# A selective-scan kernel: the skip term made in the next chunk's softplus burst, half in the first and half in the third direction, and the third pair's late sums behind its third turn

## The chip, the cores and the metric

The kernel runs on one core of a Trainium2 chip. The metric is device microseconds of one execution. TensorE (PE) multiplies matrices and turns tiles, VectorE (DVE) runs the scans, ScalarE (ACT) does exponentials and scaled copies, GpSimd (POOL) does elementwise products, SyncE (SP) issues DMAs. A product of float32 operands appears in the trace as two passes of PE, a turn (transpose) as one.

## The reference

The input has 8 images of 384 channels and 64 x 64 positions. Layer 0 normalises by groups, runs a channel attention with 1x1 and 3x3 convolutions, and adds the input. Layer 1 is a selective scan with four directions: along the rows, along the columns, and both in reverse.

```python
xs = stack([x0, x1, x0[..., ::-1], x1[..., ::-1]])      # 4 directions, 4096 steps
dts, Bs, Cs = split(einsum('bkdl,kcd->bkcl', xs, x_proj_weight))
dt = softplus(einsum('bkrl,kdr->bkdl', dts, dt_projs_weight) + dt_bias)
# for each step: h = h * exp(dt * A) + (dt * u) * B ;  y = sum over 16 states of h * C
ys = ys + Ds.reshape(K, D)[None, :, :, None] * u        # the skip term
y = y0 + y2 + yt                                        # four directions, merged in place
out = x + gelu(layer_norm(y))
```

All four directions' results are added at the same positions, so the skip term is, at each position, the normalised input times the sum of the four D's. It may be added once, whole or in parts, with any direction's results.

## The kernel before

For each image the attention runs first and then the scan. The scan works on 32 *chunks*: directions k = 0 to 3, and in each 8 pieces of 512 steps, in rising order for k of 0 and 1 and in falling order for 2 and 3. A chunk has 16 states, taken two at a time in 8 *pairs*, p = 0 to 7. Channels are three blocks of 128 partitions.

One call of `period(g)` emits the work of one pair, g counting pairs over all chunks. Everything in it is pinned, so each engine runs exactly in the order in which the Python code emits. A period holds:

- six scans on DVE (`scan`, L569: two states, three channel blocks), each fed by a decay exp(dt*A) made by ACT into PSUM (`decay`, L548, two banks) and by the drive w*B from POOL (`drive`, L557);
- for the pair before, o = g - 1: eight *turns* on PE (`turn`, L591), each three transposes of 64 steps with both states, from h into one of two PSUM banks (`ps_t`); for each turn a scaled copy out of PSUM with C as the scale (`apply_c`, L603 on ACT, L605 on DVE for some); and after every two copies a sum over the two states (`add_up`, L626 and L632), products with the constant `pair` that accumulate in `py`, three PSUM banks that live through the chunk;
- the projections of the chunk two ahead (`project`, L455), and POOL's `weigh` and `keep_last`.

Sums come in four quarters of 128 steps, lb = 0 to 3. The first three write 384 channels into the first columns of one bank each. The last (lb = 3, "late sums", twelve passes at L632) goes to the spare 128 columns of all three banks. Its eighth copy is made in the next period, after the first turn, and the sums follow behind the second turn of that next period (`add_up(o - 1, NJ)`), or behind the third turn where `odd` holds. That is the case from the third pair on when the chunk two ahead is in direction 1 or 3, whose input is read with a stride.

The second pair of a chunk, p = 1, is the *burst*. In it the step sizes of the next chunk are made: `step_matmuls` makes three products with 512 columns (L514), two in the banks of the turns and the third, pd0, in the bank `ps_m`. In front of pd0 stands a filler, a product of the same operand with the identity (L513), which pd0 overwrites. Then `step_size` runs three softplus on ACT (L524) between two changes of the activation table. In the burst three of the copies run on DVE, and DVE also takes the finished `py` of the chunk before (`take_all`: L675 copies it in direction 0, L677 adds it to the stored sums of earlier directions) before the next chunk's first sums overwrite it.

The skip term is made in direction 0 only. Twelve products per chunk (L618: a 128 x 128 block of the normalised input, times a diagonal of summed D's) are spread over the pairs by the table `SKIPS`, two with each of pairs 2 to 7, each directly in front of the sums of its quarter. Since pair p's sums are made one period later, and the late ones two periods later, the products run in the periods of p = 3 to 7 and in p = 0 of the next chunk.

```python
SKIPS = {2: (0, 1), 3: (2, 3), 4: (0, 3), 5: (1, 3), 6: (0, 2), 7: (1, 2)}
```

Of the kernel before, what the change touches and what calls it, by code (L numbers as in the profile page):

```python
# [15 lines left out]
P = 128  # L16
C = 384
NJ = C // P
H = W = 64
L = H * W  # L20
CH = 512
# [10 lines left out]
NP = N // 2  # L32
# [1 line left out]
NQ = CH // HP  # L34
PX = 4

SKIPS = {2: (0, 1), 3: (2, 3), 4: (0, 3), 5: (1, 3), 6: (0, 2), 7: (1, 2)}

FT = 256
JUNK = 512  # L40
# [36 lines left out]
def tile_channel_attention_then_selective_scan(ctx: ExitStack, tc: tile.TileContext, a: dict):  # L77
    nc = tc.nc
# [27 lines left out]
    skip = const.tile([P, NJ, P], F32, name="skip")  # L106
# [275 lines left out]
    def selective_scan(b, x1, stats1):  # L382
# [10 lines left out]
        with ExitStack() as st:  # L393
# [6 lines left out]
            pin = tc.keep_in_program_order  # L400
# [11 lines left out]
            with tc.tile_pool(name=f"sn{b}", bufs=1) as np_:  # L412
# [4 lines left out]
                for c in range(NCH):  # L417
                    for j in range(NJ):
                        s = x1[j][:, bass.ts(c, CH)]
# [20 lines left out]
            steps = []  # L440
# [59 lines left out]
                bts[g] = work.tile([P, 2, CH], F32, tag="B", bufs=3, name=f"B{b}_{g}")  # L500
                nc.sync.dma_start(bts[g], bc_ds[s][2 * p : 2 * p + 2, :].partition_broadcast(P))

            def step_matmuls(s):

                k = steps[s][0]
                pds = [None] * NJ
                for j in (1, 2, 0):
                    pool, tag = (ps_m, "m") if j == 0 else (ps_t, "t")  # L510
                    pds[j] = pool.tile([P, CH], F32, tag=tag, name=f"pd{b}_{s}_{j}")
                    if j == 0:
                        pin(nc.tensor.matmul(pds[j], lhsT=ident, rhs=xds[s], start=True, stop=True))  # L513
                    pin(nc.tensor.matmul(  # L514
                        pds[j], lhsT=wdt[:, k, bass.ts(j, P)], rhs=xds[s], start=True, stop=True
                    ))
                return pds
# [18 lines left out]
            das, dbs, h2s, hcs, pts, pys, carries = {}, {}, {}, {}, {}, {}, {}  # L536
# [70 lines left out]
            def add_up(g, lb):  # L607

                s, p = divmod(g, NP)
                if p == 0 and lb == 0:  # L610
                    pys[s] = ps_y.tile([P, NJ, CH], F32, tag="py", name=f"py{b}_{s}")
                hc, py = hcs.pop((g, lb)), pys[s]
                k, c = steps[s][:2]

                if k == 0 and lb in SKIPS.get(p, ()):
                    j = sum(lb in SKIPS[i] for i in SKIPS if i < p)
                    o = py[:, lb, bass.ts(j, P)] if lb < NJ else py[:, j, C:]
                    pin(nc.tensor.matmul(  # L618
                        o, lhsT=x1[j][:, c * CH + lb * P : c * CH + (lb + 1) * P],
                        rhs=skip[:, j, :], start=False, stop=False,  # L620
                    ))

                flags = dict(start=p == 0 and lb < NJ, stop=p == NP - 1 and lb == NJ)
                if lb < NJ:
                    for f in range(2):
                        pin(nc.tensor.matmul(  # L626
                            py[f * HP : (f + 1) * HP, lb, :C], lhsT=pair, rhs=hc[:, f, :], **flags
                        ))
                else:
                    for j in range(NJ):  # L630
                        for f in range(2):
                            pin(nc.tensor.matmul(  # L632
                                py[f * HP : (f + 1) * HP, j, C:], lhsT=pair,
                                rhs=hc[:, f, bass.ts(j, P)], **flags,
                            ))

            def rows(k, c):

# [42 lines left out]
            for s in range(2):  # L681
                for i in range(PX * NJ):
                    project(s, i)
                lay_out(s)
                if s == 0:
                    step_size(0, step_matmuls(0))
                    for j in range(NJ):
                        weigh(0, j)
                    for g in range(3):
                        fetch(g)  # L690
                    drive(0, 0)
                    drive(0, 1)
                    decay(0, 0, 0)
                    decay(0, 0, 1)
            mingle_c(0)

            def period(g):

                o, s, p = g - 1, g // NP, g % NP
                last = g == S * NP
                burst = p == 1 and s + 1 < S
                on_dve = {3, 4, 5} if burst else {0: {2}, 2: {2}}.get(p, set())
                taken = s - 1 if p == 1 and s > 0 else None

                def step(i):  # L710
                    if not last:
                        scan(g, *divmod(i, NJ))

                def next_decay(i, home=None):
                    if not last:
                        decay(g, *divmod(i + 2, NJ), home)

                def apply(q):
                    if o >= 0:
                        apply_c(o, q, nc.vector if q in on_dve else nc.scalar)  # L720

                def turned(q):
                    if o >= 0:
                        turn(o, q)

                def added(lb):
                    if o >= 0:
                        add_up(o, lb)

                def projected(i):  # L730
                    if s + 2 < S:
                        project(s + 2, i)

                def take_all():
                    if taken is not None:
                        for i in range(NJ):
                            take(taken, i)

                if not last:
                    h2s[g] = work.tile([P, NJ, CH, 2], F32, tag="h", bufs=3, name=f"h{b}_{g}")  # L740
                    if p == 2:
                        sum_of(s)
                if o >= 0:
                    keep_last(o)
                fetch(g + 3)
                drive(g + 1, 0)
                if p == 3 and s + 1 < S:
                    mingle_c(s + 1)
                if p in (2, 4, 6) and s + 1 < S:
                    weigh(s + 1, p // 2 - 1)  # L750
                turned(0)
                step(0)
                if o >= 1:
                    apply_c(o - 1, NQ - 1, nc.scalar)
                turned(1)

                odd = p >= 2 and s + 2 < S and steps[s + 2][0] % 2 == 1
                if p >= 3 or odd:
                    projected(2 * p - 4)
                if o >= 1 and not odd:  # L760
                    add_up(o - 1, NJ)
                next_decay(0)
                step(1)
                apply(0)
                turned(2)
                if o >= 1 and odd:
                    add_up(o - 1, NJ)
                next_decay(1)
                step(2)
                drive(g + 1, 1)  # L770
                apply(1)
                if burst:
                    pds = step_matmuls(s + 1)
                    apply(2)
                    next_decay(2)
                    next_decay(3, work)
                    step_size(s + 1, pds)
                    step(3)
                    step(4)
                    take_all()  # L780
                    step(5)
                    turned(3)
                    turned(4)
                    added(0)
                    apply(3)
                    turned(5)
                    apply(4)
                    turned(6)
                    added(1)
                    next_decay(4)  # L790
                    next_decay(5)
                    apply(5)
                    turned(7)
                    added(2)
                    apply(6)
                    return
                turned(3)
                if p == 1:
                    take_all()
                added(0)  # L800
                if p == 0 and 0 < s < S - 1:
                    lay_out(s + 1)
                apply(2)
                turned(4)
                next_decay(2)
                step(3)
                apply(3)
                turned(5)
                added(1)
                next_decay(3)  # L810
                step(4)
                apply(4)
                turned(6)
                apply(5)
                turned(7)
                added(2)
                if p == 2 and not odd:
                    projected(0)
                if p >= 2:
                    projected(2 * p - 3)  # L820
                if p == 0 and s < S:
                    turn_c(s)
                next_decay(4)
                step(5)
                apply(6)
                next_decay(5)
                if p == 0 and s < S:
                    keep_c(s)
# [82 lines left out]
    for b in range(B):  # L911
        x1, x1_d, stats1 = channel_attention(b, *x, before)
# [52 lines left out]
```

## Time and profile before

| | |
|---|---|
| median of 3 runs | 20747.19 us (20741.09 to 20748.04) |
| profiled execution | 20748.06 us, span 20746.3 us |
| busy, share of the span | PE 93%, DVE 93%, ACT 87%, POOL 74%, weight loads 51% |
| mean granted TensorE clock | 0.969 |
| skip products L618 | 1536 passes, 311.8 us busy |
| filler L513 | 512 passes, 263.2 us busy |
| turns L591 | 49152 passes, 7976.9 us busy, idle before them 457.5 us |
| late sums L632 | 24576 passes, 1871.6 us busy |
| scaled copies L603 on ACT | 15128, 8437.0 us busy, idle before them 346.5 us |

Length of each direction in image 1, from the first scan of one direction to that of the next (the last one ends with the first scan of its last pair): 539.67, 518.81, 514.63 and 505.57 us.

An entry "idle before, <- releaser" names the instruction whose end let the engine go on. Ends of PE's passes are modelled, so busy time of PE overlaps; starts are recorded. Times in the timeline count from the span's start.

### The profile page before, as it was taken

To read this page: it belongs to the slowest core of one execution; us is meant where nothing else is said; L and a number is where in the kernel's file an instruction comes from. 1 tells how busy PE (TensorE), PEld (TensorE's weight loads), DVE (VectorE), ACT (ScalarE), POOL (GpSimd) and SP (SyncE) were. 2 spreads that over 40 slices of the span, in tenths; PEclk is the share of its full clock that TensorE was granted. 3 is DMA by queue.
4 is the path that set the end of the run, shared out by engine and by line. 5 is a ranking of instruction groups with operands and counts; after the bars stand their busy time and mean duration, and the time that the engine had idled before them with its cause. 6 is when DMAs were issued, how large, how long until landed. Compare 5 with 4: busy or idle time off the path is not lost. (4 is left out here: it accounts for less than half of the span.)

```text
span 20746.3 us, 319602 instructions
## 1 busy us (share of the span) xinstructions
PE 19205.9 (93%) x118256; PEld 10578.6 (51%) x118256; DVE 19321.9 (93%) x17310; ACT 17951.9 (87%) x32267; POOL 15441.2 (74%) x6918
## 2 busy tenths in 40 slices
PE   7999979999899998999989999899998999989998
PEld 4555545555455554555545555455554555545554
DVE  8999989999899998999989999899998999989998
ACT  3999949999599995999859998599985999859998
POOL 0899808998189981899819997199972999729997
PEclk8999989999899998999989999899998999989999
DMA  1232322323223232232322323223232232322223
GB/s 40 76 92 92 101 77 77 92 93 101 75 80 92 92 104 70 80 92 93 105 68 80 92 92 105 70 80 92 92 103 71 81 93 92 98 74 82 92 92 117
DMA packets 953164, 1807.96 MB, mean 87 GB/s; under 512 B 125905, under 2 KB 646353, under 8 KB 945457
## 3 DMA queue, kind: packets, MB, share of 16 engines
q1 hardware_dynamic: 950736, 1787.40, 27.2%
q8 instruction: 933, 15.29, 0.3%
q14 instruction: 631, 5.16, 0.1%
q10 hardware_dynamic: 864, 0.12, 0.0%
HBM read 1468.39 MB, written 318.77 MB: 86 GB/s over the span
## 5 line engine op out<-in xcount | busy, mean ns | idle before, releaser
L557 POOL TENSOR_TENSOR db<-w,B 128x1536 f32<-128x1536 f32 x4088 | 14143.8, 3467 | 566.6 <-DVE h L569 238.8
L569 DVE TENSOR_TENSOR_SCAN h<-da,ca,db 128x512 f32<-128x512 f32 x10752 | 13058.6, 1267 | 500.2 <-issue 204.3
L603 ACT ACTIVATE hc<-pt,ct 128x384 f32<-128x384 f32 x15128 | 8437.0, 579 | 346.5 <-PE pt L591 287.5
L548 ACT ACTIVATE da<-dt,neg_a 128x512 f32<-128x512 f32 x12288 | 8504.5, 695 | 166.3 <-DVE h L569 134.2
L591 PE MATMUL pt<-ident,h 128*128 128x128 f32 x49152 | 7976.9, 287 | 457.5 <-ACT hc L603 305.0
L591 PEld LDWEIGHTS pt<-ident,h 128*128 128x128 f32 x49152 | 5145.5, 140 | 5115.7 <-ACT hc L603 2549.8
L626 PE MATMUL py<-hc,pair 128*64 128x384 f32 x24576 | 5327.1, 512 | 9.1 <-DVE ys L677 9.1
L406 POOL MEMSET wdt<- 128x1536 f32 x8 | 11.0, 1378 | 3621.5 <-DMA x1d<-x 3621.5
L569 DVE TENSOR_TENSOR_SCAN h<-da,db 128x512 f32<-128x512 f32 x1536 | 1811.5, 1231 | 145.2 <-ACT da L548 75.6
L632 PE MATMUL py<-hc,pair 128*64 128x128 f32 x24576 | 1871.6, 281 | 0.0
L626 PEld LDWEIGHTS py<-hc,pair 128*64 128x64 f32 x24576 | 1216.6, 135 | 1014.6 <-issue 945.3
L455 PE MATMUL px<-x,wx 128*44 128x128 f32 x6144 | 1501.7, 338 | 35.4 <-ACT x L421 29.1
L632 PEld LDWEIGHTS py<-hc,pair 128*64 128x64 f32 x24576 | 1377.2, 136 | 267.2 <-issue 240.2
L532 POOL TENSOR_TENSOR w<-x,dt 128x512 f32<-128x512 f32 x744 | 1057.9, 1422 | 0.0
L455 PEld LDWEIGHTS px<-x,wx 128*44 128x44 f32 x6144 | 635.0, 121 | 817.1 <-issue 771.9
L583 POOL COPY ca<-h 128x6 f32<-128x6 f32 x1792 | 344.2, 192 | 828.4 <-DVE h L569 817.2
L514 PE MATMUL pd<-xd,wdt 128*128 128x512 f32 x1536 | 781.5, 618 | 87.6 <-ACT hc L603 81.8
L605 DVE TENSOR_SCALAR hc<-pt,ct 128x384 f32<-128x384 f32 x1256 | 741.1, 607 | 106.2 <-PE pt L591 61.1
L353 PE MATMUL pp<-v,mT 128*128 128x512 f32 x1152 | 553.9, 634 | 123.5 <-DVE v L244 57.3
L524 ACT ACTIVATE dt<-pd,dt_bias 128x512 f32<-128x512 f32 x768 | 475.4, 686 | 21.3 <-PE pd L514 17.7
L514 PEld LDWEIGHTS pd<-xd,wdt 128*128 128x128 f32 x1536 | 275.3, 192 | 401.3 <-ACT hc L603 199.7
L353 PEld LDWEIGHTS pp<-v,mT 128*128 128x128 f32 x1152 | 228.3, 205 | 403.0 <-issue 312.1
(315 smaller groups left out, 11713.7 us busy)
## 6 DMA issues: line engine op xcount, KB each, us to landing
B<-bcd SPq DMA_DIRECT2D x2048, 512.0 KB
yd<-ys SPq DMA_DIRECT2D x128, 576.0 KB
ys<-yd SPq DMA_DIRECT2D x256, 288.0 KB
yd<-ys SPq DMA_DIRECT2D x256, 288.0 KB
x<-in_x SPq DMA_DIRECT2D x48, 1024.0 KB
x1d<-x SPq DMA_DIRECT2D x192, 256.0 KB
fy<-yd SPq DMA_DIRECT2D x128, 384.0 KB
fin<-yd SPq DMA_DIRECT2D x112, 384.0 KB
```

The costliest lines, as they stand in the source:

```text
L353: nc.tensor.matmul(pc, lhsT=mT[:, j, bass.ts(m, P)], rhs=v[:, j, bass.ts(c, CH)], start=j == 0, stop=j == NJ - 1,)
L455: pin(nc.tensor.matmul(split(pxs[s][:XR, :])[:, part, :], lhsT=wx[:, j, k, :], rhs=view(x1[j], k, c)[:, part, :], start=i == 0, stop=i == ...
L514: pin(nc.tensor.matmul(pds[j], lhsT=wdt[:, k, bass.ts(j, P)], rhs=xds[s], start=True, stop=True))
L532: pin(eng.tensor_mul(split(ws[s][:, j, :]), view(x1[j], k, c), split(dts[s][:, j, :])))
L548: pin(nc.scalar.activation(t, dts[s][:, j, :], AF.Exp, scale=neg_a[:, j, k, n : n + 1]))
L557: pin(eng.tensor_mul(t, ws[g // NP], bts[g][:, v : v + 1, :].broadcast_to([P, NJ, CH])))
L569: pin(nc.vector.tensor_tensor_scan(h, da, db, 0.0 if start else carries[s - 1][:, j, n : n + 1], ALU.mult, ALU.add,))
L591: pin(nc.tensor.transpose(t[:, bass.ts(j, P)], h2s[g][:, j, bass.ts(q, HP), :].rearrange("p l v -> p (l v)"), ident))
L603: pin(eng.activation(out, src, AF.Copy, scale=scale))
L605: pin(eng.tensor_scalar_mul(out, src, scale))
L626: pin(nc.tensor.matmul(py[f * HP : (f + 1) * HP, lb, :C], lhsT=pair, rhs=hc[:, f, :], **flags))
L632: pin(nc.tensor.matmul(py[f * HP : (f + 1) * HP, j, C:], lhsT=pair, rhs=hc[:, f, bass.ts(j, P)], **flags,))
```

## The change

Three things change. `SKIPS` is now keyed by direction: in direction 0 the quarters 0 and 1, in direction 2 the quarters 2 and 3. `add_up` no longer makes skip products; a new function `add_skip` makes the six of a chunk in one go. It is called in the burst of the next chunk, in front of `step_matmuls`, and where it is called, the filler in front of pd0 is left out. The accumulation's last-product flag moves with it. Lastly, `late` extends the order "late sums behind the third turn" to the third pair (p = 2) of every chunk. The number of skip products is the same, 768; the fillers fall from 256 to 128.

```diff
-SKIPS = {2: (0, 1), 3: (2, 3), 4: (0, 3), 5: (1, 3), 6: (0, 2), 7: (1, 2)}
+SKIPS = {0: (0, 1), 2: (2, 3)}
...
-            def step_matmuls(s):
+            def step_matmuls(s, filled):
...
-                    if j == 0:
+                    if j == 0 and not filled:
                         pin(nc.tensor.matmul(pds[j], lhsT=ident, rhs=xds[s], start=True, stop=True))
...
-                if k == 0 and lb in SKIPS.get(p, ()):
-                    j = sum(lb in SKIPS[i] for i in SKIPS if i < p)
-                    o = py[:, lb, bass.ts(j, P)] if lb < NJ else py[:, j, C:]
-                    pin(nc.tensor.matmul(
-                        o, lhsT=x1[j][:, c * CH + lb * P : c * CH + (lb + 1) * P],
-                        rhs=skip[:, j, :], start=False, stop=False,
-                    ))
-
-                flags = dict(start=p == 0 and lb < NJ, stop=p == NP - 1 and lb == NJ)
+                flags = dict(start=p == 0 and lb < NJ, stop=False)
+                open_ = skip_banks(k)
...
+                        flags["stop"] = p == NP - 1 and j not in open_
...
+            def skip_banks(k):
+                return {i for lb in SKIPS.get(k, ()) for i in ([lb] if lb < NJ else range(NJ))}
+
+            def add_skip(s):
+                k, c = steps[s][:2]
+                py = pys[s]
+                places = []
+                for lb in SKIPS[k]:
+                    for j in range(NJ):
+                        bank, o = (lb, py[:, lb, bass.ts(j, P)]) if lb < NJ else (j, py[:, j, C:])
+                        places.append((bank, lb, j, o))
+                for i, (bank, lb, j, o) in enumerate(places):
+                    pin(nc.tensor.matmul(
+                        o, lhsT=x1[j][:, c * CH + lb * P : c * CH + (lb + 1) * P],
+                        rhs=skip[:, j, :], start=False,
+                        stop=bank not in [q[0] for q in places[i + 1 :]],
+                    ))
...
                 odd = p >= 2 and s + 2 < S and steps[s + 2][0] % 2 == 1
+                late = odd or p == 2
                 if p >= 3 or odd:
                     projected(2 * p - 4)
-                if o >= 1 and not odd:
+                if o >= 1 and not late:
                     add_up(o - 1, NJ)
...
                 turned(2)
-                if o >= 1 and odd:
+                if o >= 1 and late:
                     add_up(o - 1, NJ)
...
                 if burst:
-                    pds = step_matmuls(s + 1)
+                    filled = taken is not None and steps[taken][0] in SKIPS
+                    if filled:
+                        add_skip(taken)
+                    pds = step_matmuls(s + 1, filled)
```

Here `taken` is the chunk before, so 16 bursts per image are filled: those of the chunks that follow one of direction 0 or 2.

More of the change, by code (lines that the diff above doesn't have):

```diff
@@ L685, in selective_scan @@
                 if s == 0:
-                    step_size(0, step_matmuls(0))
+                    step_size(0, step_matmuls(0, False))
                     for j in range(NJ):
```

## The prediction

> **What bounds the kernel now.** Most of the span is the selective scan: 2079 of some 2580 us per image. The page gives four engines 74 to 93% of the span, which names no bound, so I read the scan stage in stretches cut at the first scan of each pair. These are pairs 4, 5 and 7 (counted from 0) of a chunk of direction 0 (chunk 3 of image 1), then the same pairs of the last chunk of direction 1. Columns: length, then busy time of PE, weight loads, DVE, ACT and POOL.
>
> ```profile
> core 0: us, PE busy (x) PEld busy (x) DVE busy (x) ACT busy (x) POOL busy (x), PEclk, DMA share, GB/s
> 3307.08:3314.91 7.83, 7.69 (x58) 4.51 (x55) 7.38 (x7) 7.71 (x15) 7.83 (x3) 1.00 0.20 69
> 3314.91:3323.03 8.12, 8.12 (x60) 4.80 (x61) 7.26 (x7) 7.57 (x15) 7.39 (x6) 1.00 0.20 65
> 3331.15:3339.41 8.26, 8.26 (x60) 4.97 (x58) 7.27 (x6) 7.68 (x15) 7.13 (x5) 1.00 0.23 69
> ...
> 4096.63:4104.18 7.55, 7.29 (x54) 4.15 (x56) 7.26 (x6) 7.55 (x15) 7.55 (x3) 1.00 0.18 69
> 4104.18:4111.74 7.56, 7.31 (x54) 4.17 (x56) 7.27 (x6) 7.56 (x15) 7.41 (x4) 1.00 0.24 73
> 4119.29:4126.85 7.56, 7.31 (x54) 4.16 (x56) 7.32 (x7) 7.56 (x15) 7.31 (x3) 1.00 0.24 73
> ```
>
> In direction 1 ACT is busy for the whole period and sets it at 7.56 us. In direction 0, where the skip term lies in these periods, PE fills pairs 5 and 7, ACT has holes, and the period is 0.3 to 0.7 us longer. The timeline of pair 5 in direction 0 shows the hole (start, length, engine, instruction, idle before):
>
> ```profile
> 3318.50 0.87 PE L591 MATMUL pt<-ident,h 128*128 128x128 f32 x6
> 3319.14 0.58 ACT L603 ACTIVATE hc<-pt,ct 128x384 f32<-128x384 f32 x1 [0.55 <-PE pt L591]
> ...
> 3320.34 2.46 DVE L569 TENSOR_TENSOR_SCAN h<-da,ca,db 128x512 f32<-128x512 f32 x2 [0.63 <-ACT da L548]
> ```
>
> The fourth turn comes late behind two skip products, ACT stands 0.55 us, its next decay is late, DVE stands 0.63 us. The same place in direction 1 has PE waiting for ACT instead:
>
> ```profile
> 4107.92 0.55 PE L591 MATMUL pt<-ident,h 128*128 128x128 f32 x3 [0.17 <-ACT hc L603]
> ```
>
> Now the burst, the second pair, in direction 2:
>
> ```profile
> 4266.79 1.99 PE L514 MATMUL pd<-xd,wdt 128*128 128x512 f32 x4 [0.33 <-ACT hc L603]
> 4267.08 1.35 ACT L548 ACTIVATE da<-dt,neg_a 128x512 f32<-128x512 f32 x2
> ...
> 4268.45 1.28 ACT L524 ACT_TABLE_LOAD   x1
> 4268.61 1.02 PE L513 MATMUL pd<-xd,ident 128*128 128x512 f32 x2
> ...
> 4269.47 1.02 PE L514 MATMUL pd<-xd,wdt 128*128 128x512 f32 x2
> 4269.75 0.69 ACT L524 ACTIVATE dt<-pd,dt_bias 128x512 f32<-128x512 f32 x1
> ```
>
> The product pd0 is done at 4269.90 + 0.59 = 4270.49 and its softplus, third of three, starts at 4270.90: slack 0.41 us. pd1 and pd2 have over a microsecond. In the third pair (waits of 4273.76 to 4282.10) DVE waits for the third turn, which stands behind the late sums:
>
> ```profile
> DVE hc L605 <- PE pt L591: 0.4, 1, 0.4
> ```
>
> **What the Trainium skill says.** "TensorE: Matmul & The Clock Gate", section "Architectural detail", says that ACT and DVE are strict FIFO and PE only pulls weight loads ahead: products run in program order, so one placed early delays every turn behind it. The trace agrees (0.55 us above). "Perfetto Trace Analysis", "Identifying the Most-Contended Engine", warns that matmul busy time misleads for PE; hence I take spacings of starts, not busy times, below. "ScalarE: Activation LUTs", "What ACT_TABLE_LOAD costs", gives 1283 ns for the load and about 1380 ns for a drain; the trace has the 1283 but softplus follows within 0.02 us, so the cover in the burst is the 1.28 alone. The first page's section "HAM oscillation" warns of a lower clock after PE gaps of over some 3.4 us; the clock is 1.00 in these stretches, and the change makes no gap of PE over 0.4 us, so dropping the filler should not matter there.
>
> **The change, part by part.**
>
> *Skip products leave direction 0.* Per chunk 12 products of two passes go from pairs 2 to 7 (running in periods 3 to 7 and in period 0 of the next chunk). I compare the distances between first scans, means over images. Chunks 1 to 5 of direction 0, periods 3 to 7: 7.60, 7.82, 8.12, 8.12, 8.26, sum 39.92. The last chunk of direction 1, with the same order and layout but no skip: 7.55, 7.55, 7.55, 7.55, 7.56, sum 37.76. Gain 2.16 us; likewise about 2.17 in chunk 0. Chunks 6 and 7 project strided: 39.96 against 38.0 in direction 1's strided chunks, gain 1.96. Two products in period 0 make the next burst period late: 11.14 against 10.84 (8 times an image), gain 0.30. Per image 6 x 2.16 + 2 x 1.96 + 8 x 0.30 = 19.3; times 8 images, **155 us**.
>
> *Skip products enter 16 bursts an image* (128 in all), six each, ahead of pd1; the filler product goes. The two passes of one skip product (L618) start 0.111 us apart, and the passes of the 128x144 products of L305, which change weights from product to product as the skips will, 0.122. In the burst above the third turn's last pass starts 0.60 us before pd1, at 4266.19. The first skip pass can follow 0.11 later; eleven spacings of 0.111 and 0.20 at the change to pd1 (as from L618 to L626 today) put pd1 at 4267.72 instead of 4266.79. That is 0.93 later, of which 0.33 was PE's wait. The filler's two passes at 0.43 return 0.86, so pd0 is later by 0.07, or 0.2 at the spacing of 0.122: inside its slack of 0.41. pd1 and pd2 end about 4268.8 and 4269.7, before their softplus at 4269.75 and 4270.33. The fourth turn, right behind pd0, is later by the same; the copy that reads it starts at 4271.99, over a microsecond after. DVE's take of the sums, which must now come after the skips, starts at 4269.03, over a microsecond after their end. Central cost 0. If the cover fails: should every second pass (the one that changes to another x block) take the 0.21 us that one-column products of L136 show at most, six passes cost 0.6 more, pd0 is 0.26 past its slack, and ACT pays 0.26 x 128 = 33 us.
>
> *Third pair's late sums behind its third turn.* 16 chunks an image (those where the chunk two ahead is in direction 0 or 2, and the last two). The other chunks already have this order: their third period is 8.24 against 8.34 forward, 8.18 against 8.34 in reverse. So 8 x 0.10 + 7 x 0.16 = 1.9 us an image (the last chunk, with no burst before it, left out), 15 us in all. The cost: the third turn needs the bank of the first, whose copy on ACT ends at 4276.88, so PE stands some 0.3 us where it now works off the sums (12 passes, 0.88 us), and the fourth turn comes 0.2 later. Queued behind it are the fourth copy on ACT and a decay that today waits 0.57 us for DVE anyway. PE takes its lag into the next period, where its waits for ACT are 0.18 us. The gain: the third turn comes 0.39 earlier (4276.93 for 4277.32), for the copy on DVE that waits 0.41. I take 12 us, a little under the comparison; bounds -8 (the lag lost again) and 35 (0.29 on 120 chunks).
>
> No DMA, POOL or SP instruction moves; DVE and ACT keep their order. Sum: 20748.06 (profiled execution; span 20746.3, 1.8 around it) - 155 - 12 + 0 = **20581 us**. The median of the runs, 20747.19, is 0.9 below that execution, which is nothing here.
>
> **The rivals.**
>
> A, the forecast: 20581, own range 20550 to 20610, chance 0.70.
>
> B, the burst pays. Weight switches between different x blocks cost 0.21 and the third pair gains nothing: 20748 - 155 + 33 = 20626. For it: no such run of switching 128x128 products with 128 columns stands in the scan stage. Against: L305's flat 0.122. Chance 0.17.
>
> C, another engine holds direction 0 at part of its old length: POOL is busy through whole periods there (7.83 of 7.83). If only half the gain arrives: 20748 - 78 - 6 = 20664. Against: direction 1 with the same POOL work runs 7.55. Chance 0.07.
>
> D, slower. The twelve passes in front of the softplus pair run so slowly that softplus, and behind it every decay on ACT, waits. For a spacing s a burst pays 11s + 0.31 (into and out of the skips) - 0.60 (the old way from turn to pd1) - 0.86 (filler) - 0.41 (slack) = 11s - 1.56. It breaks even with the gain, 167/128 = 1.30 us, at s = 0.26 us. With load (0.191) and pass (0.275) unoverlapped s is 0.466, so 3.57 us x 128 = 457, less 167: 21038. Against: loads overlap everywhere in this trace (0.111 between L618's own two passes, each with its load). Chance 0.04.
>
> More gain in the third pair than bounded: 0.02, near 20545.
>
> **How the numbers follow.** Range 20545 to 20660 takes in A, B and the bounds of both unknowns; it leaves out D and most of C's far side. About 0.2% (41 us) is what a measurement here can tell from no change, 20706 to 20789. A, B, C and the last are all beyond it; C shades into it. Faster 0.93, same 0.03, slower 0.04.
>
> **What would show it.** Right: periods 3 to 7 of direction 0 near 7.55 with no ACT wait on pt; burst periods of direction 0 at 10.84 and those after direction 2 still at 10.84; the new skip line at a spacing near 0.11; ACT's softplus without a PE wait; third periods of 8.18 to 8.24 where they were 8.34, the DVE wait of 0.4 gone, the next period not over 7.6. Wrong: a wait of L524 on pd, bursts over 11.1, or direction 0's periods held up by POOL (waits on db or ca) above 7.6.

## The result, and the profile after

The changed kernel takes 20567.3 us (median, 20559.6 to 20567.6) against 20747.1 before: a ratio of 0.9913, with a 95% interval of 0.9902 to 0.9925. That is 180 us less; 20581 was forecast, 166 less.

A finer measure is the length of the scans alone, from an image's first scan to the first scan of its last pair, summed over the 8 images of the profiled execution: 16623.3 us before and 16441.8 after, 181.5 less. The rest of the span (attention, norms, and the last pair) was 4123 and 4116. In the other profiles below it lies between 4116 and 4128 without any change there, so these few microseconds mean nothing. The experiments are read by this sum, with the medians beside it. Much of its scatter is one period, the third of each image's first chunk: it takes 8.3 or 9.8 us before and 8.1 or 9.6 after, for a cause that was not looked into, and is long in 4 images of the 8 before and in 7 after. Where a few microseconds matter below, a sum *without that period* is given.

The same three pairs of a direction-0 chunk as in the prediction (chunk 3 of image 1, pairs 4, 5 and 7). Columns: length, then busy time of PE, weight loads, DVE, ACT and POOL.

```profile
core 0: us, PE busy (x) PEld busy (x) DVE busy (x) ACT busy (x) POOL busy (x), PEclk, DMA share, GB/s
3273.90:3281.45 7.55, 7.30 (x54) 4.16 (x56) 7.27 (x7) 7.55 (x15) 7.55 (x4) 1.00 0.20 69
3281.45:3289.00 7.55, 7.31 (x54) 4.16 (x56) 7.26 (x6) 7.55 (x15) 7.55 (x5) 1.00 0.19 72
...
3296.55:3304.10 7.55, 7.30 (x54) 4.15 (x56) 7.27 (x7) 7.55 (x15) 7.55 (x5) 1.00 0.21 74
```

They were 7.83, 8.12 and 8.26. ACT is now busy for the whole of each, as in direction 1 before. In the timeline of pair 5, the fourth turn waits for ACT where ACT waited 0.55 us for it:

```profile
3284.47 0.55 PE L592 MATMUL pt<-ident,h 128*128 128x128 f32 x3
3284.57 1.13 ACT L604 ACTIVATE hc<-pt,ct 128x384 f32<-128x384 f32 x2
3285.18 0.55 PE L592 MATMUL pt<-ident,h 128*128 128x128 f32 x3 [0.16 <-ACT hc L604]
```

The burst in direction 2 (chunk 2 of image 1, the chunk shown before), from the timeline after:

```profile
4219.61 1.50 PE L646 MATMUL py<-skip,x 128*128 128x128 f32 x12
4220.40 1.35 ACT L549 ACTIVATE da<-dt,neg_a 128x512 f32<-128x512 f32 x2
4220.95 2.74 PE L515 MATMUL pd<-xd,wdt 128*128 128x512 f32 x6
4222.06 1.28 ACT L525 ACT_TABLE_LOAD   x1 [0.31 <-PE pd L515]
4222.34 1.85 DVE L692 TENSOR_TENSOR ys<-ys,py 128x512 f32<-128x512 f32 x3
4223.35 1.84 ACT L525 ACTIVATE dt<-pd,dt_bias 128x512 f32<-128x512 f32 x3
```

The six products are twelve passes at a spacing of 0.111 us, with no dearer change between x blocks and none to pd1. But the table load, which waited for nothing before, now waits 0.31 us for pd1. In the program the wait for pd1 belongs to the first softplus; here it stands in front of the table load that precedes it.

It does not always stand there. In one filled burst of each image, that of direction 0's second chunk, PE runs the same order at the same times, and the load does not wait. From image 1:

```profile
3123.20 2.74 PE L515 MATMUL pd<-xd,wdt 128*128 128x512 f32 x6
3124.01 1.28 ACT L525 ACT_TABLE_LOAD   x1
3125.30 1.84 ACT L525 ACTIVATE dt<-pd,dt_bias 128x512 f32<-128x512 f32 x3
```

The load starts 0.81 us after pd1's first pass, while pd1 is still being made; in the burst above it starts 1.11 after (4222.06 - 4220.95). The trace records which semaphores ACT's instructions wait for. In this burst the first softplus waits for PE only, and that wait is its own, behind the load. In the other 120 filled bursts it waits for POOL too; then only POOL's wait is its own, and PE's is a separate instruction ahead of the load. The stretches of this burst and of the period after it:

```profile
3118.50:3129.33 10.83, 10.15 (x62) 5.67 (x62) 10.62 (x13) 10.77 (x18) 8.67 (x5) 1.00 0.39 117
3129.33:3137.44 8.11, 7.76 (x55) 4.13 (x55) 7.90 (x9) 7.28 (x14) 6.81 (x4) 1.00 0.22 77
```

The burst in direction 2 again, where the load waits, and the two periods after it:

```profile
4216.25:4227.30 11.05, 10.31 (x62) 5.75 (x62) 10.71 (x12) 10.69 (x18) 8.91 (x5) 1.00 0.40 122
4227.30:4235.12 7.82, 7.48 (x55) 4.07 (x51) 7.69 (x7) 7.40 (x14) 6.54 (x4) 1.00 0.55 167
4235.12:4242.71 7.59, 7.51 (x58) 4.48 (x58) 7.27 (x6) 7.57 (x15) 7.42 (x6) 1.00 0.20 71
```

Before they were 10.83, 8.34 and 7.49. The burst grew by 0.22, the third period fell by 0.52, the fourth grew by 0.10: 0.20 us less in all. How much of that is the burst's and how much the moved sums', the two traces can't tell, since both changes meet here. DVE's wait of 0.4 us for the third turn is gone from the list of waits.

### The profile page after: what moved, and what is told of

It is laid out like the page before. It is cut to its first block, busy times and chain, and to the rows that moved or that the text cites. A ratio compares the mean times of both kernels' runs of the same rounds, so it can differ in the third digit from the quotient of the medians.

```text
span 20557.8 us, 319218 instructions
## 1 busy us (share of the span) xinstructions
PE 19007.6 (92%) x118000; PEld 10494.5 (51%) x118000; DVE 19292.1 (94%) x17310; ACT 17927.7 (87%) x32267; POOL 15434.4 (75%) x6918
```

## The experiments

The kernel before was run again on every chip that was used, and the differences in this table are to it on the same chip. "Scans" is the sum defined above, of one profiled execution of each kernel; that of the kernel before was not taken anew on each chip.

| kernel | median us | less than before | scans us |
|---|---|---|---|
| before | 20747.1 | | 16623.3 |
| changed | 20567.3 | 179.8 | 16441.8 |
| no_skip | 20564.2 | 184.8 | 16445.2 |
| late_undone | 20583.6 | 165.3 | 16463.9 |
| split33 | 20633.7 | 115.2 | 16512.1 |
| filler_kept | 20566.9 | 182.0 | 16443.6 |
| late_alone | 20717.1 | 24.8 | 16594.2 |
| all12 | 20630.0 | 112.0 | 16509.2 |
| no_filler | 20558.9 | 183.0 | 16437.2 |
| copy_on_act | 20556.5 | 185.4 | 16435.8 |
| early_projection | 20554.1 | 188.1 | 16436.9 |
| early_and_act | 20553.8 | 188.4 | 16434.1 |
| changed_again | 20558.1 | 184.2 | 16438.4 |

The changed kernel run again, beside the last two, gives the size of what means nothing: 3 us in the scans, 4 us in the difference, 9 us in the median. Without the period that is 8.1 or 9.6 us long, its two scans sums are 16366.2 and 16365.8.

> The changed kernel as it is, on the same chip as the two runs beside it: 20567 within 10 us.

### What the six products in a burst cost

```diff
-SKIPS = {0: (0, 1), 2: (2, 3)}
+SKIPS = {}
```

> The changed kernel without any skip product (the skip term is left out; all fillers are back, the late sums stay moved). Theory 1, absorbed: the six products in a burst cost nothing in the end, since the 0.22 us by which a filled burst period grew (11.06 for 10.83) comes back in the next period. Then this runs as the changed kernel, 20567 within 8 us: burst periods 10.83, third periods back up to 8.11 and 8.18 to 8.24. Theory 2, paid: the 0.22 us in 128 bursts stays lost, and this runs 28 us shorter, near 20539.

Measured: 20564.2, and in the scans 16445.2 for 16441.8. The skip term now costs nothing that can be measured; that the fillers are back in this kernel has no weight, as the section on the filler shows. The stretches of the same burst and the two periods behind it in this kernel:

```profile
4218.89:4229.73 10.84, 9.93 (x52) 4.74 (x52) 10.63 (x13) 10.78 (x18) 8.68 (x5) 1.00 0.40 117
4229.73:4237.77 8.04, 7.70 (x55) 4.14 (x55) 7.88 (x8) 7.33 (x14) 6.77 (x4) 1.00 0.56 175
4237.77:4245.36 7.59, 7.51 (x58) 4.49 (x58) 7.26 (x6) 7.58 (x15) 7.42 (x6) 1.00 0.22 71
```

10.84 + 8.04 + 7.59 is 26.47; with the skips it was 11.05 + 7.82 + 7.59 = 26.46. What the burst loses comes back to the hundredth. ACT shows where: in the third period it is idle for 0.71 us here (8.04 - 7.33) and for 0.42 with the skips. ACT is late out of the burst, and then does without part of a wait that it has in any case. Theory 1 holds and theory 2 is out. The changed kernel shows the same by itself: the filled burst whose load does not wait takes 10.83 and the period behind it 8.11, together 18.94; in the next chunk of direction 0, whose load is 0.3 us late, it is 11.05 and 7.92, together 18.97.

### Is it ACT or DVE that sets the burst?

If ACT's delay does not count, keeping ACT on time should be worth nothing. Three of the products stay ahead of pd1 (half 0), three go to the filler's place ahead of pd0 (half 1; the lines that hand the half on are left out here):

```diff
-                        add_skip(taken)
+                        add_skip(taken, 0)
...
+                    if j == 0 and between is not None:
+                        add_skip(between, 1)
```

> The changed kernel with three skip products ahead of pd1 and three in the filler's place ahead of pd0. pd1 is then only some 0.3 us later than without skips, so ACT's table load, which waits for pd1 and had 0.45 us to spare, starts on time, and pd0 stays inside its slack: burst periods 10.83 to 10.9. Theory 1, absorbed: the third period grows back by the same, total 20567 within 8 us. Theory 2, paid: 128 times 0.22 less, near 20539.

Measured: 20633.7, and 16512.1 in the scans, 70 us more than the changed kernel. Both theories missed: both looked at ACT alone and overlooked DVE. From the timeline of the burst in this kernel:

```profile
4236.52 1.28 ACT L527 ACT_TABLE_LOAD   x1
4236.75 0.83 PE L650 MATMUL py<-skip,x 128*128 128x128 f32 x6
...
4237.62 1.88 DVE L696 TENSOR_TENSOR ys<-ys,py 128x512 f32<-128x512 f32 x3 [0.44 <-PE py L650]
```

The table load is on time, as meant. But DVE's take reads the finished `py`, and now waits 0.44 us for the later half of the skips. It starts 6.63 us into the burst (4237.62 - 4230.99), for 6.09 in the changed kernel (4222.34 - 4216.25): 0.54 later. The stretches show what becomes of it:

```profile
4230.99:4242.38 11.39, 10.19 (x62) 5.70 (x62) 10.73 (x12) 11.23 (x19) 8.69 (x5) 1.00 0.39 134
4242.38:4250.44 8.06, 7.71 (x55) 4.15 (x55) 7.89 (x9) 6.98 (x13) 6.79 (x4) 1.00 0.48 140
```

The burst is 0.55 us longer than without skips and the third period gives nothing back (8.06 for 8.04): 0.55 x 128 = 70 us, the whole difference. So in the burst 0.3 us of ACT cost nothing and 0.54 us of DVE cost all. DVE runs take, last scan and three copies one after the other, and PE's turns stand behind those copies.

The dose: all twelve products in one burst, in half as many bursts.

```diff
-SKIPS = {0: (0, 1), 2: (2, 3)}
+SKIPS = {0: (0, 1, 2, 3)}
```

> The changed kernel with all twelve skip products of a chunk in the bursts after direction 0 (64 bursts), none in direction 2. 24 passes stand ahead of pd1, so the table load comes 1.33 us later than in a burst with six. Theory 1a, DVE is the path through the burst and ACT has some 0.5 us left after six: the fourth turn's bank is freed by the first softplus, 1.33 later, DVE's copy of it comes 0.65 later, and ACT's rest of the delay is over its slack; 0.65 to 0.9 in 64 bursts, 42 to 58 us slower than the changed kernel, 20609 to 20625. Theory 1b, what ACT loses is free however late: only DVE's take waits, some 0.25 us for the skips' end, 16 us slower, 20583.

Measured: 20630.0, and 67 us more in the scans: 1.05 us for each of the 64 bursts on average. The waits of one such burst:

```profile
ACT L525 <- PE pd L515: 1.7, 1, 1.7
DVE hc L606 <- PE pt L592: 1.1, 2, 0.7
PE pt L592 <- ACT dt L525: 0.4, 1, 0.4
```

The table load is 1.7 us late. DVE, which did not feel 0.3 us, now stands 1.1 us for turns, of which the fourth needs the bank that the first softplus frees. Theory 1b is out. 1a has the mechanism, and its 42 to 58 us were too low: it counted DVE's wait for one turn, and there are two. So what is free ends somewhere between six and twelve products, and of the further 1.3 us by which the load is late, 1.1 are paid in a burst like this. Here too the first filled burst of each image is the exception: its load does not wait, only its softplus does, and it takes 11.62 us for 12.40 in the next chunk. With the period behind it, it is 0.39 us longer than in the changed kernel (19.33 for 18.94), the next chunk's 1.17 (20.14 for 18.97). So most of what twelve products cost comes through the load's place behind the wait.

### The filler

```diff
-                    pds = step_matmuls(s + 1, filled)
+                    pds = step_matmuls(s + 1, False)
```

> The changed kernel with the filler kept in the filled bursts too. pd0 comes 0.86 us later. In the changed kernel's trace its softplus starts about 0.8 us after it could, and the fourth turn, right behind pd0, has over 0.7 us before DVE reads it. If the filler's removal is what makes room for the skips (the prediction's sum: slack of pd0 0.41 us), 0.86 + 0.07 - 0.41 = 0.5 us in 128 bursts, 66 us slower, 20633. If the late table load has moved the softplus back so far that pd0 no longer counts, 0 to 15 us slower, 20567 to 20582.

```diff
-                    if j == 0 and not filled:
+                    if j == 0 and s == 0:
```

> The changed kernel with the filler gone from all bursts but the first of an image. If the filler does nothing for the time (its place is hidden behind softplus, and the clock stays at 1.00 in the bursts without it), 20567 within 8 us. If it keeps PE's clock up or fills a wait that something else then takes, unfilled bursts grow over 10.83, at 0.2 us each 24 us slower.

Measured: 20566.9 with the filler in every burst and 20558.9 with it in none (one is left at the start of each image); scans 16443.6 and 16437.2 against 16441.8 and 16438.4 for the changed kernel. Filler or not, nothing changes: without the period of 8.1 or 9.6 us, filler_kept and no_skip, run on one chip, both have 16371.0. Its removal is not what makes room for the skips: with it the filled bursts are 11.14 for 11.06 us, and the third period returns that too (7.75 for 7.82 in the chunk shown).

### The third pair's late sums

```diff
-                late = odd or p == 2
+                late = odd
```

> The changed kernel with the third pair's late sums back behind its second turn. By the sum of the prediction 12 us slower than the changed kernel, 20579. By the periods of the two traces (third and fourth period together 0.19 to 0.29 us shorter in 15 chunks an image) 23 us slower, 20590. Theory 3, the late order only makes room for the filled bursts: unfilled chunks lose 0.2 here, filled ones more, because ACT's late table load then meets late turns as well; total 30 or more, 20600.

And the reverse, the kernel before with this part alone:

> The kernel before with the third pair's late sums moved alone; skip products and fillers stay as they were. By the sum of the prediction 12 us faster than before, 20735. By the difference between the changed kernel and the one with this part undone (17 us, and 21 by the lengths of the scans in the traces), 20728. If the order helps only together with the filled bursts, no change, 20747.

Measured: undone, 20583.6, 22 us more in the scans; alone, 20717.1 (a ratio of 0.9988 to before, interval 0.9982 to 0.9995), 29 us less in the scans. Not all of the 29 is this change: in late_alone also periods in which nothing was changed are 0.06% shorter than in the trace of the kernel before. The third and fourth periods of the chunks concerned, summed over 14 chunks an image, are 23 us shorter alone and 21 us between late_undone and the changed kernel; the medians on one chip gave 25 for the part alone. It works without the filled bursts, so theory 3 and its like fall. The stretches of the third and fourth period of chunk 2 in direction 2, with this part alone:

```profile
4266.82:4274.88 8.06, 7.71 (x55) 4.16 (x55) 7.89 (x9) 7.34 (x14) 6.78 (x4) 1.00 0.58 176
4274.88:4282.46 7.58, 7.50 (x58) 4.48 (x58) 7.26 (x6) 7.56 (x15) 7.40 (x6) 1.00 0.24 71
```

8.34 and 7.49 before: 0.28 gained, 0.09 given back. In the last chunk of direction 1 it is 0.23 and 0.04.

### What sets the third period: attempts at more

After the change DVE is idle for only 0.22 us of an unfilled third period, 0.2 of them just before the next period's first scan. So its one copy went to ACT, which is idle there for 0.8 us:

```diff
-                on_dve = {3, 4, 5} if burst else {0: {2}, 2: {2}}.get(p, set())
+                on_dve = {3, 4, 5} if burst else {0: {2}}.get(p, set())
```

> The changed kernel with the third copy of the third pair on ACT instead of DVE. If DVE is what bounds the third period (in the trace of the changed kernel it stands 0.03 to 0.17 us there, ACT 0.42 to 0.84), 0.6 us leave the bound and the third period falls from 8.11 to about 7.8 in unfilled chunks and by 0.1 or nothing in filled ones: 30 to 60 us faster than the changed kernel, 20507 to 20537. If turns and copies bound it through the two banks (ACT's waits are all for turns), a copy more in ACT's queue makes every later decay late: the same or up to 25 us slower, 20567 to 20592.

Measured: 20556.5, scans 6 us shorter than the changed kernel and 3 us shorter than its second run: no change. The third period of the last chunk of direction 1, in the changed kernel and in this one:

```profile
4034.66:4042.77 8.11, 7.76 (x55) 4.15 (x55) 7.89 (x8) 7.28 (x14) 6.66 (x4) 1.00 0.29 72
...
4035.05:4043.14 8.09, 7.74 (x55) 4.14 (x55) 7.47 (x7) 7.62 (x15) 6.81 (x4) 1.00 0.32 70
```

DVE is now idle for 0.62 us of it, and it is as long as before. DVE being busy there was not DVE being the bound.

PE waits 0.35 us in the third period, for the first turn's copy. The projection fills that:

```diff
-                if p >= 3 or odd:
+                if p >= 2:
                     projected(2 * p - 4)
...
-                if p == 2 and not odd:
-                    projected(0)
```

> The changed kernel with the third pair's first projection (two passes, some 0.25 us of PE) between its second and third turn in every chunk, as chunks with strided projections have it, instead of at the period's end. Theory 4, PE sets the third period: the copy moved to ACT left its length at 8.09 for 8.11, so neither DVE nor ACT bounds it, and PE stands 0.35 us before the third turn, which waits for the first turn's copy. The projection fills that wait and its time at the end is saved: third period 0.2 to 0.25 us shorter in 13 chunks an image (those with a chunk two ahead in direction 0 or 2), 21 to 26 us faster than the changed kernel. Theory 5, something else sets the third period (the chain from turn to copy to decay to scan): the projection delays the third turn by up to 0.1 and nothing is gained, within 8 us or up to 10 slower.

> The same with the third pair's third copy on ACT too. If PE is the bound by itself, the same as with the projection alone, within 8 us. If PE and DVE bound the third period together, each hiding the other, both gains show only here: 20 us or more below the projection alone.

Measured: 20554.1 and 20553.8, beside 20558.1 for the changed kernel on that chip; scans 1.5 and 4 us shorter. PE's wait did vanish (0 for 0.35), and the third period is 8.11 as before; in direction 2 the fourth fell from 7.58 to 7.52. Theory 4 falls. The sums keep their place (they start 3.64 us into the period either way), because the third turn before them waits for the first turn's bank and starts at the same moment. What fits is theory 5, a chain through the two turn banks: turn, copy on ACT, the next turn. It is the theory left over and was not tested by itself. None of these versions is distinguishable from the changed kernel.

## Why the prediction was right, and where its steps were not

**Skips out of direction 0: right.** Forecast 155 us. Between late_alone and the changed kernel the scans shrink by 152 us (16594.2 to 16441.8), which includes the skips' cost in the bursts, nothing; without the period of 8.1 or 9.6 us it is 155. Periods 4 to 7 of direction 0 are 7.55 us, as read off direction 1. Reading one direction's stage as the price of the other without the term was sound: without the skips the two do the same work in the same order, and they now take the same time.

**Skips into the bursts: the sum right, its reason wrong.** The step that failed is "pd1 and pd2 end ... before their softplus". It set the time at which softplus begins against pd1's end and found 1.28 us of cover in the table load. That holds only for the first filled burst of an image, which does take the forecast 10.83. In the other 120 of 128 the load itself waits for pd1. Its slack was 0.45 us (pd1 could be read at about 4268.0 in the burst of before, the load began at 4268.45), and pd1 came some 0.75 later. So a softplus that was to be on time is 0.3 late there, and the forecast of bursts at 10.84 us missed: they take 11.06. A wait for pd at this place was one of the prediction's own signs of being wrong, and it came. The total still came out, and that was luck: the cover was one that the prediction never named, ACT's waits for turns in the third period. no_skip shows the return, split33 that ACT's time is not what counts, all12 where it ends. The filler, whose 0.86 us the sum took as return, plays no part.

**Late sums: right way, about half the size.** Forecast 12 us, measured 21 to 25. The term was read off the chunks with strided projections, third periods of 8.24 and 8.18. Those have a projection between the second and third turn and read it with a stride. The chunks in question have neither, and fell to 8.11 and 8.05. early_projection tells which of the two counts: a projection there without a stride leaves the third turn at 3.17 us into the period and the period at 8.11. In the strided chunks of direction 1 the third turn starts at 3.30, and the period is longer by the same 0.13 (8.24). The lag behind was as feared in kind: the fourth period grew by 0.04 to 0.10, inside the bounds.

**The rivals.** B (skips at 0.21 us a pass) fell with the spacing of 0.111. C (POOL holds direction 0) fell with periods of 7.55 in which POOL is as busy as ACT. D (slower) would have needed s = 0.26. With all12's 24 passes its formula gives 23 x 0.111 - 1.56 = 0.99 us a burst, close to the 1.05 measured, but the agreement is chance: the formula charges what is left over pd0's slack, and by it filler_kept should have lost 0.5 us a burst and lost nothing.

The forecast of the whole was 14 us high. The late sums account for some 10 of them, and what is left is no more than two runs of one kernel differ here.

## What to carry to other kernels

When products are moved in front of a function that needs a new activation table, look in the trace where the wait for them stands. Here it stood ahead of the table load in 120 bursts of 128, and the slack ended at the load, not at the function. In a stage where several engines are over 90% busy, find the engine whose delay is paid by delaying one at a time: here 0.3 us on ACT came back in the next period and 0.54 us on DVE did not, with both engines busy for 97% of the burst. And a period that becomes longer is no loss until the sum with the next ones has been taken.

## What the runs showed of the hardware

- Where the wait for PE was an instruction of its own, it came ahead of the table load: ACT waited 0.31 us (six products) and 1.7 us (twelve) for pd1, and only then loaded for 1.28. Where the softplus waited for PE alone, the load ran first, at 5.51 us into the burst for 5.81, with pd1 arriving at the same time.
- Twelve float32 passes with another 128 x 128 block of weights at every product run 0.111 us apart, no slower than the two passes of one product, with weight loads of 0.19 us each hidden.
- Leaving out the filler did not lower PE's clock: the mean granted clock was 0.968 in the runs with it in every burst, and 0.968 or 0.969 in those without it.
